# Unequal chunks in a fused Mamba and mixture-of-experts kernel, and zero rows only where they are read

## The chip, the cores and the metric

The kernel runs on one core of one Trainium2 chip. The metric is device time in microseconds (us). A core has five engines with queues of their own: TensorE (PE, matrix products; its weight loads are listed as PEld), VectorE (DVE), ScalarE (ACT), GpSimd (POOL) and SyncE (SP), which issues most of the DMA transfers here. An engine works through its own instructions in order and waits for others at semaphores. SBUF is the on-chip memory with 128 partitions, PSUM the small memory into which PE writes.

## What is computed

The input `x` is 4 sequences of 1024 tokens of 256 values. Two layers follow, each with a residual and a layer norm. The first is a selective state-space layer (512 channels, 16 states per channel), the second a mixture of experts: one shared expert for all tokens, and 8 experts of which each token takes the best 2.

```python
# first layer: x = layernorm(x + attn(x)), where attn adds x once more
h = x * rsqrt(mean(x * x) + EPS) * norm_scale
xs, res = split(h @ w_in, 2)                   # 2 x 512 channels
res = silu(res)
xs = silu(causal_depthwise_conv(xs, conv_w, conv_b))   # 4 taps
delta, B, C = split(xs @ w_xproj, [16, 32])
delta = softplus(delta @ w_dt + b_dt)
deltaA = exp(delta[..., None] * A)
deltaBx = (delta * xs)[..., None] * B[:, :, None, :]
ys = scan over tokens: ys[t] = deltaA[t] * ys[t - 1] + deltaBx[t]
out = (einsum('blcn,bln->blc', ys, C) + xs * D) * res
x = layernorm(x + (x + out @ w_out))
# second layer: x = layernorm(x + ffn(x))
normed = x * rsqrt(var + 1e-08) * norm_weight
shared = relu(normed @ sw1 + sb1) @ sw2 + sb2
probs = sigmoid(flat @ router_w.T)
scores, idx = top_k(probs, 2)                  # of 8; weights: scores over their sum
routed = sum over the two experts e of weight * (relu(flat @ ew1[e] + eb1[e]) @ ew2[e] + eb2[e])
x = layernorm(x + shared + routed)
```

## The kernel before

**Chunks.** A sequence is cut into chunks (b, c) of `TC` = 512 tokens, eight in all. Each goes through three stages.

`front` (line 248) normalises the tokens, turns them so that channels lie on partitions (`hT`), projects them (`pi`), convolves (line 298 on ACT, then three taps each for four channel blocks on DVE, line 304), and works out `delta`, `xs * delta` and the rows of B and C (`parts`). For the second chunk of a sequence, the last three columns of the chunk before come in through `halo`.

The scan runs one state n at a time, 16 steps for a chunk (the loop from line 926). A step has these parts: `inputs` multiplies `xs` by B (DVE line 406 for three channel blocks, POOL line 410 for the fourth); for each of four channel blocks k, `scan` lets ACT make `da` (line 418) in one of two PSUM buffers, and DVE scans along the tokens (line 421), from zero or from the state that `keep` saved; `outputs` multiplies by C (DVE line 434) and adds up over n (POOL line 435).

`tail` (line 438) multiplies by the gate, projects back (`po`, line 458), adds the residual, normalises, writes the result to the DRAM array `sums`, and routes: the router's product, the top two of eight and their weights. `by_expert` then counts with two matrix products where each token's row belongs, and POOL scatters rows (values, weight, token number) into the DRAM array `rows` with indirect DMAs (line 596), where each expert has a stretch of its own. Last it makes a `plan`: which experts have full blocks of 128 rows, and where they begin. `channels` marks a chunk whose shared work can begin, `routes` one whose plan is there.

**Units of expert work.** `units` (line 662) is a fixed list: for each chunk one unit for each 128 tokens of the shared expert, then `BLOCKS` routed units. How many tokens each expert has is not known when the program is built, so the numbers are those that any routing can fill: 1, 8, 8, 8, 8, 8, 8, and for the last chunk the rest, 22. With the shared ones, four for each chunk, that makes 103. A unit loads its expert's weights (two of 1 MB, `need`, two buffers each), its rows (`load_rows`, line 713; rows after an expert's last token must hold zeros and a harmless token number), turns them, multiplies by the first weights (`up`, line 768), takes Relu on ACT (line 777), multiplies by the second (`down`, line 798), and adds its 128 rows into `sums` with an indirect DMA (line 830). Which expert, and where its rows begin, are read from `plan` into SyncE's registers (lines 695 and 722). `fill` writes zero rows over all of `rows` once, 1806 KB in each DMA, beginning at step 2 of the first chunk.

**Order.** The order in which instructions enter the queues is written out by hand with Python generators. `front` of the next chunk and `tail` of the one before are advanced by `side()`, twice in each step; that is 32 turns in a chunk, whatever its length. Expert work `moe()` (line 838) is advanced by `other_work()` 0.85 times for each k, four k to a step; a unit takes four turns (two in `up`, two in `down`), and the `up` of a unit comes ahead of the `down` of the one before. Turns that find nothing ready are lost. After the last scan the remaining units run with two turns to each turn of the last tail, and `finish` (line 873) normalises `sums` and writes the output.

Of the kernel before, what the change touches and what calls it, by code (L numbers as in the profile page):

```python
# [22 lines left out]
TC = 512  # L23
NCH = SEQ // TC
TT = TC // P
# [14 lines left out]
GROUP = NSEQ * NCH  # L40
NGROUP = NSEQ * NCH // GROUP
CAP = GROUP * TC
FULL = TC * TOPK // BS


BLOCKS = [FULL * k + FULL - (E - 1) for k in range(GROUP - 1)] + [FULL * GROUP + E - 1]
BLOCKS = [after - (BLOCKS[k - 1] if k else 0) for k, after in enumerate(BLOCKS)]
NB = max(BLOCKS)
# [3 lines left out]
NS = NB * BS + E * CAP  # L52
# [5 lines left out]
def mamba_moe_kernel(  # L58
# [32 lines left out]
    def load_x(b, c):  # L91
        t = two.tile([P, TT, D], F32, tag="x", name=f"x_{b}_{c}", bufs=3)
        nc.sync.dma_start(t, x[b, c * TC : (c + 1) * TC, :].rearrange("(t p) d -> p t d", p=P))
        return t
# [62 lines left out]
    nc.vector.tensor_scalar(starts, steps[:, 0:E], float(CAP), float(NB * BS), ALU.mult, ALU.add)  # L157
# [11 lines left out]
    halo = const.tile([P, KB, K - 1], F32, tag="halo", name="halo")  # L169


    rows_of, sums_of = [], []
    for g in range(NGROUP):
        rows_of.append(dram.tile([NS, W], F32, tag=f"rows{g}", name=f"rows{g}", bufs=1))
        sums_of.append(dram.tile([P + GROUP * TC, D], F32, tag=f"sums{g}", name=f"sums{g}", bufs=1))

    empty = one.tile([P, W], F32, tag="o", name="empty")
# [5 lines left out]
    def fill(g):  # L183

        nc.sync.dma_start(sums_of[g][0:P, :], empty[:, 0:D])
        rows = rows_of[g].rearrange("(n p) d -> p n d", p=P)
        for n in range(0, NS // P, 14):
            some = min(14, NS // P - n)
            nc.sync.dma_start(
                rows[:, n : n + some, :], empty.unsqueeze(1).to_broadcast([P, some, W])  # L190
            )
            yield
# [23 lines left out]
    def to_channels(hn, which, dst, name):  # L216

        for k in range(KD):
            pt = ps_mix.tile([P, TC], F32, tag="mix", name=f"pt_{name}_{k}")
            for t in range(TT):  # L220
                nc.tensor.transpose(
                    pt[:, t * P : (t + 1) * P], hn[:, t, k * P : (k + 1) * P], ident
                )
            yield
            nc.scalar.activation(
                dst[:, k, :], pt, AF.Identity, scale=norms_sb[:, which, k : k + 1]
            )
# [15 lines left out]
    chunks = [(b, c) for b in range(NSEQ) for c in range(NCH)]  # L243

    sofar_of, done_of = {}, {}


    def front(b, c):
        s = f"{b}_{c}"
        x_sb = xs_in[b, c]  # L250
# [44 lines left out]
        for k in range(KB):  # L295
# [5 lines left out]
            )  # L301
            for back in range(1, K):
# [4 lines left out]
            if c + 1 < NCH:  # L307
                nc.scalar.copy(halo[:, k, :], pi[:, TC - (K - 1) :])
            yield
        if c > 0:  # L310
            come = one.tile([P, KB, K - 1], F32, tag="come", name=f"come_{s}")
# [76 lines left out]
    def over_partitions(step, row):  # L388

        b, c, n = step  # L390
        pb = ps_mix.tile([P, TC], F32, tag="mix", name=f"pb_{b}_{c}_{row}")
# [8 lines left out]
    def inputs(step, pb):  # L400
        b, c, n = step
        xs = scans[b, c][0]
# [10 lines left out]
    def scan(step, hs, of):  # L413
        b, c, n = step
        delta = scans[b, c][1]
# [10 lines left out]
    def keep(step, hs):  # L426
        b, c, n = step
        if c + 1 < NCH:
            nc.scalar.copy(state[:, :, n : n + 1], hs[:, :, TC - 1 : TC])  # L429

    def outputs(step, hs, pb):
        b, c, n = step
        y = scans[b, c][2]
        nc.vector.tensor_tensor(hs, hs, pb.unsqueeze(1).to_broadcast([P, KB, TC]), ALU.mult)  # L434
# [3 lines left out]
    def tail(b, c):  # L438
        s = f"{b}_{c}"
        g, at = divmod(chunks.index((b, c)), GROUP)  # L440
        own_sums = sums_of[g][P + at * TC : P + (at + 1) * TC, :]
# [35 lines left out]
        for _ in range(3):  # L477
# [4 lines left out]
            base=P + at * TC, channel_multiplier=1,  # L482
# [3 lines left out]
        yield  # L486
        x1T = one.tile([P, KD, TC], F32, tag="x1T", name=f"x1T_{s}")
# [3 lines left out]
        pr = ps_mix.tile([P, TC], F32, tag="mix", name=f"pr_{s}")  # L491
# [13 lines left out]
        den, flat = part(TT), part(TT * E * E)  # L505
# [18 lines left out]
        tie = flat.rearrange("p (t e f) -> p t e f", t=TT, e=E)  # L524
# [26 lines left out]
        if at:  # L551
            nc.gpsimd.tensor_copy(sofar[:, 0, :], sofar_of[g][:, TT, :])
        else:
            nc.gpsimd.memset(sofar[:, 0, :], 0.0)
        sofar_of[g] = sofar
# [9 lines left out]
        yield from by_expert(b, c, hn, rank, weights, both, part, flat)  # L565

    def by_expert(b, c, hn, rank, weights, both, part, flat):

        s = f"{b}_{c}"
        g, at = divmod(chunks.index((b, c)), GROUP)  # L570
        blocks, last_of_group = BLOCKS[at], at == GROUP - 1
# [3 lines left out]
        nc.tensor.matmul(place, lhsT=ones, rhs=sofar_of[g], start=True, stop=False)  # L575
# [17 lines left out]
        def scatter(i):  # L593
            nc.gpsimd.tensor_copy(hn[:, :, WEIGHT : WEIGHT + 1], weights[:, i, :].unsqueeze(2))
            for t in range(TT):
                ins = nc.gpsimd.indirect_dma_start(  # L596
                    rows_of[g][:, :],
# [5 lines left out]
                for other in taken_from[g]:  # L603
                    tc.declare_no_dep(ins, other, reason="rows behind those of full blocks")
                scatters.append(ins)


        if not at:
            done_of[g] = one.tile([P, E], F32, tag="done", name=f"done_{g}")
            nc.gpsimd.memset(done_of[g], 0.0)  # L610
        done = done_of[g]
        levels = [P, E, CAP // BS]
        over = one.tile(levels, F32, tag="ahead", name=f"over_{s}")
        level = full_at[:, 0 : CAP // BS] if last_of_group else full_at[:, 1:]
        nc.vector.tensor_tensor(
            over, counts.unsqueeze(2).to_broadcast(levels),
            level.unsqueeze(1).to_broadcast(levels), ALU.is_gt if last_of_group else ALU.is_ge,
# [9 lines left out]
        base, ends, first, whose, first_of = part(E), part(E), part(E), part(blocks), part(blocks)  # L627
        nc.vector.tensor_reduce(base, ee, AX.X, ALU.add)
# [19 lines left out]
        nc.vector.tensor_reduce(first_of, of, AX.X, ALU.add)  # L648
        plan = two.tile([P, 2, blocks], I32, tag="plan", name=f"plan_{s}")
        nc.vector.tensor_scalar(plan[:, 0, :], whose, float(E - 1), None, ALU.min)  # L650
        nc.vector.scalar_tensor_tensor(
            plan[:, 1, :], step, float(BS), first_of, ALU.mult, ALU.add
        )
        if not last_of_group:
# [8 lines left out]
    for i, (b, c) in enumerate(chunks):  # L663
        units += [(b, c, SHARED, j) for j in range(TC // BS)]
        units += [(b, c, None, j) for j in range(BLOCKS[i % GROUP])]
# [6 lines left out]

    def group(u):
        return chunks.index(units[u][0:2]) // GROUP
# [36 lines left out]
    blocks_in, rows_in, taken_from = {}, {}, [[] for _ in range(NGROUP)]  # L711
# [3 lines left out]
    def load_rows(u):  # L715
# [4 lines left out]
        g = group(u)  # L720
# [3 lines left out]
        ins = nc.sync.dma_start(xb, rows_of[g][bass.ds(first, BS), :]).ins  # L724
# [6 lines left out]
        taken_from[g].append(ins)  # L731
# [58 lines left out]
    def down(u, hidden):  # L790
        b, c, e, j = units[u]
        g, at = divmod(chunks.index((b, c)), GROUP)
# [11 lines left out]
        if e is not None:  # L804
# [4 lines left out]
            )  # L809
            if j % 2 == 0:  # L810
# [3 lines left out]
            if j % 2:  # L814
                first = P + at * TC + (j - 1) * BS

                def add():
                    nc.gpsimd.dma_start(
                        sums_of[g][first : first + 2 * BS, :].rearrange("(t p) d -> p t d", p=P),
# [9 lines left out]
        def add():  # L829
            nc.gpsimd.indirect_dma_start(  # L830
                sums_of[g][:, :],
# [6 lines left out]
    def moe():  # L838

        while not ready(0):  # L840
            yield False
        ahead = []
        for _ in up(0, ahead):
            yield True
        for u in range(last):
            while u + 1 < last and not ready(u + 1):
                while pending:
                    pending.pop(0)()
                yield False
# [23 lines left out]
    def finish(g):  # L873

        while pending:
            pending.pop(0)()
# [145 lines left out]
```

## Time and profile before

| | us |
|---|---|
| median of 3 runs | 1759.77 (1757.38 to 1762.43) |
| the profiled execution | 1759.7 |
| its span | 1758.0 |
| start of the first scan instruction | 71.7 |
| start of the first scan of each later chunk | 224.9, 406.7, 574.4, 754.7, 935.3, 1115.5, 1291.1 |
| end of the last scan instruction | 1452.2 |
| end of the last unit's `down` | 1703.6 |
| busy: PE, DVE, ACT, POOL | 1266.4, 1285.8, 1098.3, 1159.2 |

The profile is of one execution. A group line gives the source line, engine, operation, what is written and read with its shape, how often, then the busy time of the group, the mean length of one in ns, and the idle time of the engine just before these instructions, with what ended it. A stretch line gives a window from the span's start, its length, the busy time of each engine in it, TensorE's granted clock, the DMA engines' share and their GB/s. The length of an instruction is not the distance to the next: neighbours on one engine overlap by some 0.1 us.

### The profile page before, as it was taken

What the parts mean: (1) busy time and instruction counts of PE and PEld (TensorE: products, weight loads), DVE (VectorE), ACT (ScalarE), POOL (GpSimd) and SP (SyncE); (2) the same over time, 40 slices, a digit from 0 to 9 for tenths busy, and PEclk for the clock granted to TensorE, in tenths of its full rate; (3) what the DMA queues carried; (4) which work ended last, traced back from release to release, by engine and by line L of the source; (5) the groups of instructions that cost most, each with busy time, mean ns of one, the idle gap of its engine ahead of it and who ended that gap; (6) DMA issues with size and microseconds to landing.
All of it is one profiled execution on the core that took longest, in us unless ns stands there. A gap on an engine that the chain in (4) does not pass through costs nothing.

```text
span 1758.0 us, 20275 instructions
## 1 busy us (share of the span) xinstructions
PE 1266.4 (72%) x6366; PEld 968.6 (55%) x6366; DVE 1285.8 (73%) x1369; ACT 1098.3 (62%) x2413; POOL 1159.2 (66%) x901
## 2 busy tenths in 40 slices
PE   4254245874677788788777977898788788999970
PEld 1011022652256657675566655776567677899960
DVE  2499889889998897999888979897989892100003
ACT  5557636684688587857775778677866663344433
POOL 1565876697678877996688768966897683312222
PEclk9575566786789998899988988899789899999995
DMA  9990000220115551564246524651555276599974
GB/s 295 323 318 31 0 5 20 68 68 0 27 50 163 150 158 45 153 179 143 64 142 169 167 61 123 190 156 46 160 168 156 55 233 190 153 313 319 331 234 159
DMA packets 199998, 254.18 MB, mean 145 GB/s; under 512 B 21306, under 2 KB 177091, under 8 KB 199891
## 3 DMA queue, kind: packets, MB, share of 16 engines
q1 hardware_dynamic: 173858, 222.54, 39.8%
q0 software_dynamic: 17648, 21.96, 7.0%
q10 hardware_dynamic: 8384, 8.39, 1.4%
q8 instruction: 50, 0.82, 0.2%
q14 instruction: 58, 0.47, 0.1%
HBM read 185.67 MB, written 67.20 MB: 144 GB/s over the span
## 4 chain that ended last, share of the span: by engine, by line
PE 16%; DVE 12%; POOL 9%; issue 6%; DMA 4%; ACT 3%; ACTq 0%; SPq 0%; POOLq 0%; DVEq 0%
PE pu L768 7%; PE pd L798 6%; DVE hs L421 6%; POOL y L435 3%; DMA sums<-rb,xb 2%; DVE hs L434 2%; DVE hs L406 2%; PE po L458 2%; POOL rows L596 1%; POOL hs L410 1%; DVE xs L304 1%; DMA sums<-rs 1%; POOL delta L377 1%; DMA rows<-hn,to 1%; ACT h L777 1%
## 5 line engine op out<-in xcount | busy, mean ns | idle before, releaser
L435 POOL TENSOR_TENSOR y<-y,hs 128x2048 f32<-128x2048 f32 x128 | 592.7, 4631 | 139.3 <-DVE hs L434 127.9
L418 ACT ACTIVATE da<-delta,chan_sb 128x512 f32<-128x512 f32 x512 | 352.9, 695 | 175.9 <-DVE hs L421 170.7
L798 PE MATMUL pd<-w,h 128*128 128x256 f32 x1648 | 402.4, 388 | 19.8 <-ACT rs L813 11.2
L798 PEld LDWEIGHTS pd<-w,h 128*128 128x128 f32 x1648 | 310.5, 195 | 92.5 <-issue 27.3
L421 DVE TENSOR_TENSOR_SCAN hs<-da,state,hs 128x512 f32<-128x512 f32 x256 | 317.9, 1269 | 27.7 <-ACT da L418 27.4
L421 DVE TENSOR_TENSOR_SCAN hs<-da,hs 128x512 f32<-128x512 f32 x256 | 302.9, 1208 | 28.2 <-ACT da L418 24.1
L768 PEld LDWEIGHTS pu<-xT,w 128*128 128x128 f32 x2272 | 287.0, 202 | 64.5 <-ACT xT L751 39.9
L777 ACT ACTIVATE h<-pu,wb 128x128 f32<-128x128 f32 x824 | 237.0, 368 | 121.9 <-PE pu L768 117.4
L768 PE MATMUL pu<-xT,w 128*128 128x128 f32 x2272 | 290.9, 286 | 22.7 <-ACT xT L751 21.9
L434 DVE TENSOR_TENSOR hs<-hs,pb 128x2048 f32<-128x2048 f32 x128 | 290.4, 2268 | 6.1 <-ACT state L429 4.6
L406 DVE TENSOR_TENSOR hs<-xs,pb 128x1536 f32<-128x1536 f32 x128 | 222.0, 1735 | 33.2 <-POOL xs L383 17.8
L830 POOL DMA_INDIRECT sums<-rb,xb x71 | 112.4, 1584 | 185.1 <-ACT xT L751 49.6
L392 PE MATMUL pb<-parts,pick 128*128 128x512 bf16 x256 | 108.8, 430 | 172.0 <-DVE hs L406 80.6
L410 POOL TENSOR_TENSOR hs<-xs,b 128x512 f32<-128x512 f32 x128 | 177.4, 1390 | 64.7 <-ACT b L404 63.6
L274 PE MATMUL pi<-hT,w_in_sb 128*128 128x512 f32 x256 | 151.6, 724 | 48.9 <-DVE hs L434 18.0
L768 PEld LDWEIGHTS pu<-x1T,w 128*128 128x128 f32 x1024 | 152.7, 230 | 32.8 <-issue 16.6
L768 PE MATMUL pu<-x1T,w 128*128 128x128 f32 x1024 | 158.8, 317 | 12.8 <-ACT h L777 12.8
L213 DVE BATCH_NORM_STATS2 bnst_l<-o 128x6 f32<-128x256 f32 x32 | 11.9, 412 | 190.8 <-DMA o<-sums 190.8
L274 PEld LDWEIGHTS pi<-hT,w_in_sb 128*128 128x128 f32 x256 | 52.8, 224 | 134.4 <-issue 47.3
L458 PE MATMUL po<-w_out_sb,y 128*128 128x256 f32 x256 | 78.6, 474 | 47.7 <-POOL y L447 42.0
L392 PEld LDWEIGHTS <-pick 128*128 128x128 bf16 x256 | 27.1, 107 | 133.3 <-issue 83.4
L458 PEld LDWEIGHTS po<-w_out_sb,y 128*128 128x128 f32 x256 | 61.6, 246 | 70.5 <-POOL y L447 49.1
(161 smaller groups left out, 1418.3 us busy)
## 6 DMA issues: line engine op xcount, KB each, us to landing
w<-in_ew SPq DMA_DIRECT2D x142, 1024.0 KB
rows<-empty SPq DMA_DIRECT2D x19, 1806.0 KB
w<-in_sw SPq DMA_DIRECT2D x16, 1024.0 KB
xb<-rows SPq DMA_DIRECT2D x71, 129.0 KB
x<-in_x SPq DMA_DIRECT2D x8, 512.0 KB
sums<-summed ACTq DMA_DIRECT2D x8, 512.0 KB
sums<-rs POOLq DMA_DIRECT2D x16, 256.0 KB
o<-sums SPq DMA_DIRECT2D x4, 1024.0 KB
```

Source lines behind the costliest of these rows:

```text
L274: nc.tensor.matmul(pi, lhsT=w_in_sb[:, k, m * P : (m + 1) * P], rhs=hT[:, k, :], start=(k == 0), stop=(k == KD - 1),)
L392: nc.tensor.matmul(pb, lhsT=pick[:, row : row + 1].to_broadcast([P, P]), rhs=scans[b, c][3], start=True, stop=True,)
L406: nc.vector.tensor_tensor(hs[:, 0:on_pool, :], xs[:, 0:on_pool, :], pb.unsqueeze(1).to_broadcast([P, on_pool, TC]), ALU.mult,)
L410: nc.gpsimd.tensor_tensor(hs[:, on_pool, :], xs[:, on_pool, :], copy, ALU.mult)
L418: nc.scalar.activation(da, delta[:, k, :], AF.Exp, scale=chan_sb[:, k, CA + n : CA + n + 1])
L421: nc.vector.tensor_tensor_scan(hs[:, k, :], da, hs[:, k, :], 0.0 if c == 0 else state[:, k, n : n + 1], ALU.mult, ALU.add,)
L434: nc.vector.tensor_tensor(hs, hs, pb.unsqueeze(1).to_broadcast([P, KB, TC]), ALU.mult)
L435: nc.gpsimd.tensor_tensor(y, y, hs, ALU.add)
L458: nc.tensor.matmul(po[:, i, :], lhsT=y[:, k, t * P : (t + 1) * P], rhs=w_out_sb[:, k, :], start=(k == 0), stop=(k == KB - 1),)
L768: nc.tensor.matmul(pu[:, i, :], lhsT=w[:, k, at : at + P], rhs=xT[:, k, :], start=(k == 0), stop=(k == KD - 1),)
L777: nc.scalar.activation(t[:, i, :], pu[:, i, :], AF.Relu, bias=wb[:, m : m + 1])
L798: nc.tensor.matmul(pd, lhsT=hidden[h][:, i, :], rhs=w[:, m, :], start=(m == 0), stop=(m == HB - 1 and e is None),)
```

## The change

- Chunks have lengths of their own: 256, 256, 512 in the first sequence, 512, 512 in the second and third, 512, 256, 256 in the last. There are ten. Tiles, loops and views take the chunk's length. `BLOCKS` becomes 0, 1, 8, 8, 8, 8, 8, 8, 4, 18. The sum with the shared units stays 103. `halos` has two buffers, and the halo copy stands ahead of the DVE taps.
- `fill` writes only one block of zero rows (for units that have none) and the padding rows of `sums`. After the last chunk's counts are known, eight DMAs write 128 zero rows each behind each expert's last row, at places that SyncE reads from `gaps`. Each expert's stretch has 128 rows more (`STRIDE`).
- A chunk without routed blocks scatters its rows and makes no plan. A plan's unused units point to the first block (`there_is`).
- `other_work` is advanced by 0.85 times the chunk's share of 512 for each k. `moe` begins the next unit's `up` ahead only if that unit is ready, and does not hold the present one back for it. A tail makes its `x1T` only when the shared units of the chunk before have been emitted (`shared_left`).
- `load_x` for chunk place + 2 stands in the middle of chunk `place`; before, that for place + 1 stood at its beginning.

```diff
+CHUNKS = [(256, 256, 512), (512, 512), (512, 512), (512, 256, 256)]
+LEN, FIRST = {}, {}
+for _b, _lens in enumerate(CHUNKS):
+    for _c, _len in enumerate(_lens):
+        LEN[_b, _c], FIRST[_b, _c] = _len, sum(_lens[:_c])
+MAXC = max(LEN.values())
...
-BLOCKS = [FULL * k + FULL - (E - 1) for k in range(GROUP - 1)] + [FULL * GROUP + E - 1]
-BLOCKS = [after - (BLOCKS[k - 1] if k else 0) for k, after in enumerate(BLOCKS)]
-NB = max(BLOCKS)
+BLOCKS, _so_far = {}, 0
+for (_b, _c), _len in LEN.items():
+    _blocks = (_b * SEQ + FIRST[_b, _c] + _len) * TOPK // BS
+    _after = max(_blocks - (E - 1), 0) if _blocks < TOKENS * TOPK // BS else _blocks + E - 1
+    BLOCKS[_b, _c], _so_far = _after - _so_far, _after
+NB = max(BLOCKS.values())
...
-    def fill(g):
-
-        nc.sync.dma_start(sums_of[g][0:P, :], empty[:, 0:D])
-        rows = rows_of[g].rearrange("(n p) d -> p n d", p=P)
-        for n in range(0, NS // P, 14):
-            some = min(14, NS // P - n)
-            nc.sync.dma_start(
-                rows[:, n : n + some, :], empty.unsqueeze(1).to_broadcast([P, some, W])
-            )
-            yield
+    def fill():
+
+        nc.sync.dma_start(rows_of[0:BS, :], empty)
+        nc.sync.dma_start(sums_of[0:P, :], empty[:, 0:D])
...
+            if c + 1 < len(CHUNKS[b]):
+                nc.scalar.copy(halos[:, c % 2, k, :], pi[:, TC - (K - 1) :])
             for back in range(1, K):
...
-            if c + 1 < NCH:
-                nc.scalar.copy(halo[:, k, :], pi[:, TC - (K - 1) :])
...
+        while shared_left:
+            yield
+        shared_left.extend(range(TC // BS))
         x1T = one.tile([P, KD, TC], F32, tag="x1T", name=f"x1T_{s}")
...
+        if last_chunk:
+
+            gaps = one.tile([P, E], I32, tag="gaps", name="gaps")
+            nc.vector.tensor_tensor(gaps, counts, starts, ALU.add)
+            for e in range(E):
+                where = nc.sync.value_load(gaps[0:1, e : e + 1], min_val=BS, max_val=NS - BS)
+                ins = nc.sync.dma_start(rows_of[bass.ds(where, BS), :], empty).ins
...
+        if not blocks:
+            scatter(0)
+            yield
+            scatter(1)
+            routes[b, c] = (scatters, None)
+            return
...
+        nc.vector.tensor_scalar(there_is, whose, float(E), float(BS), ALU.is_lt, ALU.mult)
+        nc.vector.tensor_tensor(there_is, step, there_is, ALU.mult)
...
-        while not ready(0):
-            yield False
-        ahead = []
-        for _ in up(0, ahead):
-            yield True
+        hidden = {}
         for u in range(last):
-            while u + 1 < last and not ready(u + 1):
-                while pending:
-                    pending.pop(0)()
-                yield False
+            if u not in hidden:
+                while not ready(u):
+                    while pending:
+                        pending.pop(0)()
+                    yield False
+                hidden[u] = []
+                for _ in up(u, hidden[u]):
+                    yield True
...
-            if u + 1 < last:
-                for _ in up(u + 1, ahead):
+            if u + 1 < last and ready(u + 1):
+                hidden[u + 1] = []
+                for _ in up(u + 1, hidden[u + 1]):
                     yield True
...
-    def other_work():
+    def other_work(share):
         nonlocal owed
-        owed += at_once
+        owed += at_once * share
...
-                        if place + 1 < len(chunks):
-                            xs_in[chunks[place + 1]] = load_x(*chunks[place + 1])
...
+                if n == N // 2 and place + 2 < len(chunks):
+                    xs_in[chunks[place + 2]] = load_x(*chunks[place + 2])
...
-            other_work()
+            other_work(LEN[b, c] / MAXC)
```

## The prediction

> **What bounds the kernel now.** I first read the 40 slices of the page: VectorE (DVE) is at 8 or 9 tenths up to slice 32, then nearly idle, and TensorE (PE) is at 9 only after that. So there are two regimes: a scan that DVE carries, then a stretch of expert work that PE carries. I then looked up the first and last scan instruction (line 421) of each chunk in the timeline and asked for busy time between those points. One row per stretch; the columns are length, busy time of PE, its weight loads, DVE, ACT, POOL, then clock and DMA:
>
> ```profile
> 72.00:225.00 153.00, 56.29 (x88) 16.64 (x86) 145.08 (x115) 88.84 (x150) 100.93 (x38) 0.59 0.45 134
> 225.00:407.00 182.00, 113.22 (x402) 73.93 (x403) 160.29 (x162) 111.72 (x209) 128.90 (x108) 0.73 0.13 39
> ...
> 574.00:755.00 181.00, 146.59 (x757) 116.31 (x756) 160.08 (x163) 130.78 (x285) 146.88 (x108) 0.90 0.45 133
> ...
> 1115.00:1291.00 176.00, 149.04 (x755) 116.78 (x754) 155.23 (x160) 125.38 (x277) 140.08 (x89) 0.89 0.45 133
> 1291.00:1452.00 161.00, 132.15 (x739) 111.18 (x738) 144.93 (x141) 100.53 (x230) 128.68 (x84) 0.90 0.51 150
> 1452.00:1704.00 252.00, 242.21 (x1608) 223.06 (x1606) 16.31 (x49) 105.52 (x345) 64.52 (x67) 0.99 0.85 262
> 1704.00:1758.00 54.00, 0.00 (x0) 0.00 (x0) 15.21 (x72) 17.20 (x37) 12.72 (x57) 0.54 0.50 158
> ```
>
> The first five rows shown are scans of one chunk of 512 tokens: DVE is busy all but 8 us of the first, 22, 21, 21 and 16 us of the others. In the sixth, PE is busy 242 of 252 us. In the last only the final norm runs. Before 72 us the first chunk's front runs alone. So the span is 72 + 1380 + 252 + 54 = 1758 us, and the profiled execution took 1759.7 (1.7 us lie outside the span), which is the median, 1759.77, within 0.1 us.
>
> Inside the scan I read two of its steps in the DVE timeline (start, length, instruction):
>
> ```profile
> 95.25 2.26 DVE L434 TENSOR_TENSOR hs<-hs,pb 128x2048 f32<-128x2048 f32 x1
> 97.43 2.33 DVE L421 TENSOR_TENSOR_SCAN hs<-da,hs 128x512 f32<-128x512 f32 x2
> 99.68 1.73 DVE L406 TENSOR_TENSOR hs<-xs,pb 128x1536 f32<-128x1536 f32 x1
> 101.33 2.33 DVE L421 TENSOR_TENSOR_SCAN hs<-da,hs 128x512 f32<-128x512 f32 x2
> 103.57 2.26 DVE L434 TENSOR_TENSOR hs<-hs,pb 128x2048 f32<-128x2048 f32 x1
> ```
>
> From start to start a step costs 2.18 + 2.25 + 1.65 + 2.24 = 8.3 us, 133 us for 16 steps. From the groups of instructions by shape (count, busy us, mean ns, idle before):
>
> ```profile
> L418 ACT ACTIVATE da<-delta,chan_sb 128x512 f32<-128x512 f32 x512 | 352.9, 695 | 175.9 <-DVE hs L421 170.7 <-issue 1.6 <-ACT summed L236 0.9
> L421 DVE TENSOR_TENSOR_SCAN hs<-da,state,hs 128x512 f32<-128x512 f32 x256 | 317.9, 1269 | 27.7 <-ACT da L418 27.4
> L421 DVE TENSOR_TENSOR_SCAN hs<-da,hs 128x512 f32<-128x512 f32 x256 | 302.9, 1208 | 28.2 <-ACT da L418 24.1 <-POOL hs L410 3.5
> L777 ACT ACTIVATE h<-pu,wb 128x128 f32<-128x128 f32 x824 | 237.0, 368 | 121.9 <-PE pu L768 117.4 <-ACT b L404 1.4 <-issue 1.1
> ```
>
> A scan that takes up a state costs 61 ns more. Last, the chain of waits in the PE stretch:
>
> ```profile
> 1685.05 3.57 PE pu L768 x32
> ...
> 1692.30 3.57 PE pu L768 x32
> ```
>
> One routed unit of expert work (a block of 128 rows) comes every 7.25 us there.
>
> **Step 1, the zero rows: 0 us.** Twenty large writes `rows<-empty`, 36.7 MB, go. They land by 135 us, beside the first chunk's scan, where DVE lacks 8 us in all, mostly behind ACT. The first scatter into these rows is at 325 us. Nothing waits for them; the bound is a gain of those 8 us.
>
> **Step 2, lead-in: -24 us.** The first front shrinks to 256 tokens. On its chain to the first scan at 72 us, these pieces scale with tokens: squares and scaling 3.4, transposes and hT 3.4, projection and convolution 13.2, Silu 1.9, pp 5.7, the pz loop 12.3, Ln 1.9, delta on POOL 4.5, y 2.6, xs on POOL 4.5, the first inputs 3.4: 57 us. Half is 28; less 4 for per-instruction cost that does not shrink. Bounds -20 and -26.
>
> **Step 3, DVE work in the scan: +39 us.** Two 512 chunks become four of 256, so 128 steps become 160, on the engine that bounds. Lengths 2048 and 1536 start 2.18 and 1.65 us apart: 1.035 ns an element and 0.06 us fixed. The trace has scans of one length only; pure proportion gives 0.56 us at 256, ACT's fixed share (below) 0.69; I take the elementwise 0.06, so 0.59, as the same engine does it. A short step is then 1.12 + 0.86 + 4 x 0.59 = 4.34 us, 69.4 for 16, against 66.6 for half a long chunk: +11 for four. Two more short chunks take up state: 128 x 0.06 = +8. Fronts: the first row's 145 less 133 is 12 us for a long front; a short one 7.4 (half, and fixed parts). Before, seven long fronts lie in the scan, after it six long and three short: +10. Tails: the chunk without a front has 145 - 137 = 8; a short one, mostly tiny router operations, 6. Seven long against six long and three short: +10. Sum 39; bounds 30 and 65 (scans at 0.69).
>
> **Step 4, DVE's waits: +29 us.** In the first and last sequence DVE now lacks 8 + 22 + 21 + 16 = 67 us. These waits come with events of a front or tail (ACT's convolution input 29 us over the run, POOL's xs 18, the router's POOL step 19), and with ACT's `da` (51). The events become more: nine fronts for seven. And ACT has less slack: from 695 and 368 ns, 0.85 ns an element and 0.26 us fixed, so `da` at 256 costs 0.48 us, 64 of them 8.5 us more than half. In chunk (3,1), with a long chunk's tail, a short front and 6.8 units of experts, I sum ACT to 31 `da` + 10 copies + 22 experts + 9 tables + 20 front and tail = 92 us, beside DVE's 89. I put the waits at 8, 19, 20 and 20, 17, 12 us in the six chunks: 96, so +29. Bounds: nothing, if waits shrink with the chunk, and +70, if ACT and DVE mostly fail to overlap in short chunks.
>
> A rule speaks against short chunks here. The row: 59 table loads on ACT at 1283 ns (7.4 a chunk); at 28.20 us one starts right after the instruction before it, and the Silu starts at 29.50, so a switch costs 1.30 us. The Trainium skill, "ScalarE: Activation LUTs", section "What ACT_TABLE_LOAD costs", adds a drain of 1380 ns, about 2.66 us for each switch. Fifteen more loads are 19 us of ACT by the row, 40 by the rule; in (3,1) ACT would stand at 102 us, above DVE, and the sum would rise by some 20 us. The row decides: 1.30.
>
> **Step 5, the end: -20 us.** The last chunk has 2 + 18 units for 4 + 22, but all 103 are still done, and how many lie before the scan's end is a matter of turns: a unit takes four, a long chunk gives 64 x 0.85 = 54, a short one 27. Following the generators' yields, 70 units are done before and 72 after. That is two, not six: chunk (3,0)'s twelve come ready halfway through (3,1), behind six of (2,1), and five of them and all six of (3,1) are left too. Two units are 14.5 us; the last tail's PE work (32 `po` matmuls, transposes, router: 12 us) halves, -6. Bounds -28 and -8.
>
> **Step 6, waits added: +1 us.** The eight gap writes need SyncE register loads that wait for `gaps` from DVE; queued behind on SyncE are the weight loads of the next units. Two buffers of each weight are two units, 14.5 us, of cover; 8 x (0.57 load + 0.4 issue) = 8 us fit. Without the cover 8 us, once. The last chunk's row loads wait for these writes, but already waited for scatters (until 1531 us), and there are four scatters instead of eight. Shared weights for two more chunks are 4 MB, at a DMA share of 0.45. The check on `shared_left` holds back (3,1)'s tail two steps, with experts to do. The earlier load of x saves only 2.9 us of ACT wait, seen once, at the start. The halo copy ahead of the taps, the unit that no longer waits for its successor, and one more small DVE operation a chunk: within 2 us together.
>
> Sum: -24 + 39 + 29 - 20 + 1 = +25, on 1759.7: **1785 us**.
>
> **Rivals.** A (0.52): as summed; 1770 to 1805. B (0.20): DVE's waits are a share of time, not of events; step 4 gives +3, the total 1759. For it: many waits are for token-sized work (POOL's 4.6 us `y`). Against: chunks with a tail lose 20 us whatever their neighbours. C (0.20): in (0,1), which carries a long front, and (3,1), ACT, DVE and POOL near 90 us each come one after another in place of beside; +70 in step 4, total 1826 at most, 1812 likely. D (0.08), the faster side: the waits halve in short chunks, because each is the remainder of a token-sized POOL or ACT operation. Then 3 + 9 + 19 and 19 + 9 + 7 = 66, no growth; with lead-in -26, end -25 and DVE at +36, the total is 1745. It decides where DVE's idle time in these six chunks stays under 70 us. That the change does not do what it says can show only in the end stretch: if 32 units or more are left after the last scan, as now, step 5 is zero.
>
> **How the numbers follow.** About 0.3%, 5 us, is what a measurement can tell from no change. A and C are slower; B is split, two parts in three within 5 us or faster; D is faster. Faster 0.10, same 0.12, slower 0.78. The range reaches from B and part of D to most of C: 1754 to 1813.
>
> **What would show it.** Right: first scan at 48 us; `rows<-empty` down to small writes; scans of 256 near 0.67 us long; chunk (3,1) near 106 us and (0,1) near 110; last scan near 1496; 30 or 31 units after it. Wrong: DVE idle under 70 us in the six chunks, scans of 256 far from 0.67 us, or an end stretch under 215 us.

## The result: slower by 3.5%, and the profile after

The kernel before takes 1758.58 us (median), the changed one 1820.94: ratio 1.0354 [1.0331, 1.0377]. The direction was forecast; the time lies 36 us above the forecast of 1785 and 8 above the range. The profiled execution has a span of 1817.8 us. The rows below are the stretches of the changed kernel, one row for each of its ten chunks from first scan to first scan, then from the last scan to the last unit, and the final norm (columns as before):

```profile
50.50:137.30 86.80, 33.94 (x83) 16.72 (x82) 76.35 (x114) 59.01 (x146) 55.03 (x43) 0.58 0.00 0
137.30:251.80 114.50, 65.44 (x222) 36.83 (x223) 92.50 (x142) 81.37 (x182) 76.05 (x82) 0.71 0.10 23
251.80:424.00 172.20, 87.34 (x273) 47.62 (x272) 160.92 (x160) 104.38 (x184) 120.98 (x92) 0.71 0.10 29
424.00:598.50 174.50, 119.60 (x530) 80.83 (x530) 156.73 (x165) 120.15 (x249) 134.33 (x96) 0.81 0.25 75
598.50:785.90 187.40, 153.04 (x745) 118.29 (x745) 166.85 (x164) 127.68 (x276) 140.24 (x105) 0.86 0.42 126
785.90:971.10 185.20, 148.54 (x761) 114.51 (x760) 160.38 (x165) 132.37 (x298) 145.94 (x104) 0.90 0.45 132
971.10:1155.40 184.30, 149.07 (x742) 114.72 (x741) 161.69 (x164) 126.66 (x271) 142.44 (x106) 0.87 0.42 124
1155.40:1321.50 166.10, 135.44 (x732) 112.70 (x733) 150.15 (x164) 117.25 (x285) 134.90 (x106) 0.90 0.46 137
1321.50:1439.60 118.10, 91.93 (x513) 76.31 (x511) 92.54 (x164) 84.68 (x231) 89.58 (x88) 0.88 0.43 125
1439.60:1534.10 94.50, 76.32 (x438) 63.56 (x437) 79.00 (x138) 66.78 (x176) 66.23 (x70) 0.91 0.49 146
1534.10:1763.10 229.00, 222.21 (x1465) 203.30 (x1464) 12.23 (x47) 95.52 (x314) 55.13 (x58) 0.99 0.90 279
1763.10:1817.80 54.70, 0.00 (x0) 0.00 (x0) 15.20 (x72) 17.50 (x37) 12.82 (x57) 0.52 0.50 156
```

The same stretches of both kernels (us; "lead-in" is the time to the first scan, and the middle is the second and third sequence):

| stretch | before | after | difference | forecast |
|---|---|---|---|---|
| lead-in | 71.7 | 50.5 | -21.2 | -24 |
| first sequence | 335.0 | 373.5 | +38.5 | +68 with the last |
| four chunks in the middle | 708.8 | 731.4 | **+22.6** | **0** |
| last sequence | 336.7 | 378.7 | +42.0 | (above) |
| last scan to last unit | 251.4 | 229.0 | -22.4 | -20 |
| final norm | 54.4 | 54.7 | +0.3 | 0 |

The differences sum to the 59.8 us between the spans. The surprise is the third row: those chunks have 512 tokens in both kernels. The short steps are as forecast. In the DVE timeline of chunk (0,0):

```profile
79.21 0.94 DVE L410 TENSOR_TENSOR hs<-xs,pb 128x768 f32<-128x768 f32 x1
80.07 1.21 DVE L438 TENSOR_TENSOR hs<-hs,pb 128x1024 f32<-128x1024 f32 x1
81.20 1.26 DVE L425 TENSOR_TENSOR_SCAN hs<-da,hs 128x256 f32<-128x256 f32 x2
82.38 0.45 DVE L308 SCALAR_TENSOR_TENSOR xs<-pi,chan_sb,xs 128x255 f32<-128x255 f32 x1
```

From start to start these are 0.86, 1.13 and 2 x 0.59 us, where 0.86, 1.12 and 0.59 were taken. The groups by shape (count, busy us, mean ns, idle before):

```profile
L425 DVE TENSOR_TENSOR_SCAN hs<-da,state,hs 128x256 f32<-128x256 f32 x192 | 136.5, 736 | 27.7 <-ACT da L422 16.9 <-POOL hs L414 8.4 <-POOL y L439 1.9
L422 ACT ACTIVATE da<-delta,chan_sb 128x256 f32<-128x256 f32 x256 | 120.1, 479 | 37.4 <-DVE hs L425 35.3
L425 DVE TENSOR_TENSOR_SCAN hs<-da,hs 128x256 f32<-128x256 f32 x64 | 41.2, 675 | 6.7 <-ACT da L422 6.5
```

Scan, 61 ns for the state, and `da` at 0.48 us are the forecast's figures. In the end stretch's chain the units are 7.25 us apart, as before:

```profile
1693.78 3.57 PE pu L789 x32
...
1701.03 3.57 PE pu L789 x32
```

The zero rows are gone: nine writes of 129 KB in place of 36.7 MB. In the middle, DVE's largest wait has grown. First the changed kernel, then, by the same view, the kernel before (line waited for, us, times, longest):

```profile
DVE hs L425 <- ACT da L422: 43.0, 19, 5.0
```

```profile
DVE hs L421 <- ACT da L418: 26.3, 18, 3.8
```

That is not all of it, as DVE's busy time there has grown too, from 632.1 to 645.7 us, though its work is the same. Part of this is standing that the profile counts as work. In the timeline of the changed kernel:

```profile
667.07 4.52 POOL L439 TENSOR_TENSOR y<-y,hs 128x2048 f32<-128x2048 f32 x1 [5.35 <-DVE hs L438]
...
668.68 2.93 DVE L200 TENSOR_SCALAR root_r<-half_r 128x4 int32<-128x4 int32 x1
```

The operation on four elements a partition lasts here until POOL's `y` ends at 671.6. Its group, and that of the operation ahead of it (min, median, longest in ns), show that such lengths are the exception:

```profile
L198 DVE TENSOR_SCALAR half_r<-ms x10: 141/160/4499, 5.0 to 1216.9; 128x4 int32<-128x4 int32 x6, 128x2 int32<-128x2 int32 x4
L200 DVE TENSOR_SCALAR root_r<-half_r x10: 135/163/2986, 5.2 to 1226.5; 128x4 int32<-128x4 int32 x6, 128x2 int32<-128x2 int32 x4
```

I call DVE instructions of at most 64 elements a partition that last over 1 us "standing" and add them up for the four middle chunks (us):

| kernel | length | DVE's other work | standing | idle | of it for `da` |
|---|---|---|---|---|---|
| before | 708.8 | 629.1 | 3.0 | 76.7 | 26.3 |
| after | 731.4 | 632.7 | 12.9 | 85.7 | 43.0 |
| order alone (e4, below) | 727.5 | 633.1 | 5.9 | 88.5 | 42.8 |
| change, order held (f4) | 682.0 | 630.2 | 11.1 | 40.7 | 19.1 |
| equal, held (g1) | 711.4 | 632.7 | 11.3 | 67.4 | 25.5 |
| equal, held, plan mended (h2) | 709.4 | 633.1 | 3.0 | 73.4 | 26.4 |
| first short, held, plan mended (i1) | 687.8 | 629.3 | 12.5 | 45.9 | 21.5 |

The work is the same everywhere, within 4 us. Of the 22.6 us, standing has 9.9 and idle time 9.0. Which edits did it is the question for the runs; how much of the standing is a cost of its own is seen at h2.

### The profile page after: what moved, and what is told of

Same layout as the page of the kernel before. It is cut to its first block, busy times and chain, and to the rows that moved or that the text cites. A ratio compares the mean times of both kernels' runs of the same rounds, so it can differ in the third digit from the quotient of the medians.

```text
span 1817.8 us, 21573 instructions
## 1 busy us (share of the span) xinstructions
PE 1298.7 (71%) x6534; PEld 994.7 (55%) x6534; DVE 1335.6 (73%) x1679; ACT 1164.6 (64%) x2721; POOL 1192.6 (66%) x1066
## 4 chain that ended last, share of the span: by engine, by line
PE 19%; POOL 17%; DVE 14%; issue 8%; DMA 5%; ACT 4%; SPq 0%; POOLq 0%; ACTq 0%; DVEq 0%
POOL y L439 7%; PE pd L818 7%; PE pu L789 7%; DVE hs L425 6%; DVE hs L438 3%; DMA sums<-rb,xb 3%; PE po L463 2%; DVE hs L410 2%; POOL hs L414 2%; POOL sums L851 1%; POOL y L452 1%; POOL rows L604 1%; ACT da L422 1%; DMA sums<-rs 1%; POOL delta L380 1%
## 5 line engine op out<-in xcount | busy, mean ns | idle before, releaser
L439 POOL TENSOR_TENSOR y<-y,hs 128x2048 f32<-128x2048 f32 (+1 forms) x160 | 603.2, 3770 | 167.0 <-DVE hs L438 152.0
L422 ACT ACTIVATE da<-delta,chan_sb 128x512 f32<-128x512 f32 (+1 forms) x640 | 385.3, 609 | 157.5 <-DVE hs L425 153.6
L818 PE MATMUL pd<-w,h 128*128 128x256 f32 x1648 | 423.3, 401 | 39.4 <-ACT h L798 22.4
L425 DVE TENSOR_TENSOR_SCAN hs<-da,state,hs 128x256 f32<-128x256 f32 (+1 forms) x384 | 374.7, 1002 | 53.1 <-ACT da L422 42.0
L438 DVE TENSOR_TENSOR hs<-hs,pb 128x2048 f32<-128x2048 f32 (+1 forms) x160 | 294.9, 1843 | 16.5 <-ACT state L433 13.7
L425 DVE TENSOR_TENSOR_SCAN hs<-da,hs 128x512 f32<-128x512 f32 (+1 forms) x256 | 268.8, 1075 | 39.3 <-ACT da L422 33.4
L798 ACT ACTIVATE h<-pu,wb 128x128 f32<-128x128 f32 x824 | 236.5, 370 | 88.1 <-PE pu L789 76.7
L396 PE MATMUL pb<-parts,pick 128*128 128x512 bf16 (+1 forms) x320 | 120.8, 380 | 196.8 <-DVE hs L410 90.6
L410 DVE TENSOR_TENSOR hs<-xs,pb 128x1536 f32<-128x1536 f32 (+1 forms) x160 | 226.2, 1414 | 30.4 <-POOL y L439 13.0
L414 POOL TENSOR_TENSOR hs<-xs,b 128x512 f32<-128x512 f32 (+1 forms) x160 | 190.9, 1197 | 68.5 <-ACT b L408 65.7
L276 PE MATMUL pi<-hT,w_in_sb 128*128 128x512 f32 (+1 forms) x320 | 159.1, 630 | 43.7 <-DVE hs L438 13.7
L408 ACT COPY b<-pb 128x512 f32<-128x512 f32 (+1 forms) x160 | 80.7, 505 | 57.2 <-PE pb L396 51.2
```

Of the source, the lines that this page charges most:

```text
L276: nc.tensor.matmul(pi, lhsT=w_in_sb[:, k, m * P : (m + 1) * P], rhs=hT[:, k, :], start=(k == 0), stop=(k == KD - 1),)
L396: nc.tensor.matmul(pb, lhsT=pick[:, row : row + 1].to_broadcast([P, P]), rhs=scans[b, c][3], start=True, stop=True,)
L410: nc.vector.tensor_tensor(hs[:, 0:on_pool, :], xs[:, 0:on_pool, :], pb.unsqueeze(1).to_broadcast([P, on_pool, TC]), ALU.mult,)
L414: nc.gpsimd.tensor_tensor(hs[:, on_pool, :], xs[:, on_pool, :], copy, ALU.mult)
L422: nc.scalar.activation(da, delta[:, k, :], AF.Exp, scale=chan_sb[:, k, CA + n : CA + n + 1])
L425: nc.vector.tensor_tensor_scan(hs[:, k, :], da, hs[:, k, :], 0.0 if c == 0 else state[:, k, n : n + 1], ALU.mult, ALU.add,)
```

## The experiments

Ratios are to the kernel before, with 95% intervals; "middle" is the four middle chunks, 709 us before.

**Which edit.** Theory 1 was that edits without a size cost the middle its 22 us; the rival, that the short chunks push the middle too. Four runs take the change apart: all edits with equal chunks; short chunks in the first, or the last, sequence alone; and the kernel before with the new `moe` alone.

```diff
-CHUNKS = [(256, 256, 512), (512, 512), (512, 512), (512, 256, 256)]
+CHUNKS = [(512, 512)] * 4                                             # e1
+CHUNKS = [(256, 256, 512), (512, 512), (512, 512), (512, 512)]        # e2
+CHUNKS = [(512, 512), (512, 512), (512, 512), (512, 256, 256)]        # e3
```

> All edits of the change, but eight equal chunks of 512 as before. Theory 1 (the four long chunks in the middle, which lost 22 us in the changed kernel, lose them to the other edits: the order of the expert work, the halo copy, the router's extra operations): every chunk loses some 5 us here too, 1758 + 8 x 5 = 1798 us, between 1785 and 1805. Rival (the short chunks push the middle too, by shifting what lies beside what): nothing of it here, 1753 to 1765 us.

1791.11 us, 1.0165 [1.0127, 1.0202]; middle 735. This is in the range of theory 1: about half of the net loss is there with equal chunks. Its middle has 20.6 us of standing.

> All edits, but only the first sequence has short chunks (256, 256, 512). By the trace of the changed kernel the first scan starts 21 us sooner and the first sequence's scan takes 38 us more: +17. Theory 1 adds some 5 us for each of the six other chunks: 1758 + 17 + 30 = 1805 us. The rival (short chunks push the middle) gives 1758 + 17 + 22 = 1797, with the last sequence as before. Short chunks that cost nothing but the two terms: 1775.

1818.6 us, 1.0305 [1.0267, 1.0343]; middle 735. This is above both expectations.

> All edits, but only the last sequence has short chunks (512, 256, 256). By the trace of the changed kernel the last sequence takes 42 us more and the end stretch 22 less: +20. Theory 1 adds 5 us for each of the six chunks ahead: 1758 + 20 + 30 = 1808 us. The rival gives the middle nothing, since no short chunk lies ahead of it: 1778.

1795.19 us, 1.0182 [1.0146, 1.0217]. This lies between the two expectations, but the middle takes 728 us though no short chunk lies ahead of it, which speaks against the rival. With this order a short beginning costs 27 us over e1, a short end 4.

> The kernel before with one edit: the expert generator does not hold a unit back for its successor, and begins the next unit ahead only when it is ready. If this edit is what the middle chunks lose time to: 1775 to 1798 us. If the halo copy or the router's operations are: within 5 us of 1758. If it helps, because the last unit of a chunk is not held back: 1745 to 1753.

1790.03 us, 1.0158 [1.012, 1.0196]; middle 727.5, with 42.8 us of waits for `da`, as in the changed kernel (43.0). The order alone loses about what e1 loses:

```profile
DVE hs L421 <- ACT da L418: 42.8, 21, 5.3
```

Of the 30 us between its span and that of the kernel before, 19 lie in the middle (12 of them idle time of DVE), 7 in the last sequence and 5 behind the last scan.

**Undoing the order.** In the new order a chunk's last routed unit finishes at once, and the `up` of the next chunk's first shared unit no longer lies ahead of its `down`. Holding it back again, with all else of the change kept (the old order also held a chunk's last shared unit; this edit does not):

```diff
         for u in range(last):
...
+            while units[u][2] is None and u + 1 < last and not ready(u + 1):
+                while pending:
+                    pending.pop(0)()
+                yield False
             for v in range(u + 1, u + 3):
```

> The whole change, but the last routed unit of a chunk is again held back until the next chunk's first unit is ready. If the expert order is worth its 28 us here too: 1821 - 28 = 1793 us, 1784 to 1800, which is the forecast's sum for the short chunks. If the short chunks have a phase of their own, in which the order does not matter: 1810 to 1825.

1770.96 us, 1.0059 [1.0038, 1.008]: 50 us less than the change, more than the 28 that were expected. First and last sequence and the end stretch keep their lengths within some 4 us each; the middle falls from 731 to 682:

```profile
426.00:590.30 164.30, 116.75 (x493) 77.48 (x494) 154.65 (x165) 117.73 (x238) 132.16 (x96) 0.82 0.24 73
590.30:766.10 175.80, 146.71 (x781) 116.47 (x780) 165.64 (x166) 128.42 (x285) 146.61 (x107) 0.92 0.47 140
766.10:934.60 168.50, 140.65 (x724) 108.37 (x725) 155.86 (x163) 127.37 (x287) 139.07 (x101) 0.92 0.46 137
934.60:1108.00 173.40, 144.06 (x781) 113.97 (x780) 165.14 (x166) 127.10 (x279) 146.76 (x107) 0.94 0.48 141
```

```profile
DVE hs L425 <- ACT da L422: 19.1, 11, 3.3
```

DVE's idle time there is 41 us for 86, with work and standing within 3 us of the change's. So what the order costs here is waiting, and the wait that shrinks most is the one for `da`, 43.0 to 19.1.

The same with equal chunks, and with only the last sequence short:

> All edits of the change with the held unit put back, and eight equal chunks of 512. Theory S (the short chunks cost what the steps of the forecast say, some +19 in the first and +17 in the last sequence by the trace of the run with both; the other edits help the middle by 27 us): 1771 - 36 = 1735 us, 1725 to 1745, below the kernel before. Rival (the middle is fast only because short chunks lie before it): 1755 to 1765, and the short chunks cost 9 us in all.

1761.38 us, 1.0007 [0.9995, 1.0019]. The time is the rival's, not theory S's 1735. The order costs 30 us with equal chunks, 50 with short ones.

> The same, with short chunks in the last sequence alone. Theory S: 1735 + 17 = 1752 us, 1742 to 1760. Rival: as the kernel before, 1758 to 1770.

1781.81 us, 1.0146 [1.0102, 1.0191]: above both expectations, and more than with both ends short. The prices of the two ends don't add up.

**Is it the place?** On e4's kernel two empty turns between the two `up`s, or ahead of the first; on the kernel before, the same two turns after the hold:

```diff
+                if u:
+                    yield True
+                    yield True
```

> The kernel before with the new expert order, and two turns left empty after the first unit's up in each chunk, where the old order had the held unit's down. All later units then stand at the same steps as in the old order; only the held unit itself is done early. Theory P (the new order is slow because everything after stands two turns, 0.6 of a step, sooner): back to 1755 to 1766 us. Theory H (the held unit's down fills PE where the next chunk's first units wait for ACT and for weights): stays at 1782 to 1795, or grows, as two turns more are lost.

1779.53 us, 1.0108 [1.0081, 1.0136]. The middle is back at 701 us, but the last chunk takes 180.5 us for 161, 14.0 of it waits for `da`.

> The same two empty turns, but ahead of the first unit's up. Theory P: like the other, 1755 to 1768 us. Theory H: 1782 to 1800. If only the distance between the first unit's up and the second's counts (ACT must clear two PSUM buffers in between): this one stays slow, 1780 or more, and the one with the gap in between gets fast.

1781.45 us, 1.0105 [1.0078, 1.0132]; middle 711, last chunk again 180.6. Both times lie between theory P and theory H, this one at the edge of H.

> The kernel before, old order, with two empty turns after each hold: all expert work after it stands two turns later. If the time depends on where the turns fall among the steps (the kernel sits at a good place, and any shift costs): 1770 to 1795 us, like the new order. If the step at which expert work stands does not matter: 1758, plus at most 2 units more after the last scan, 1758 to 1768.

1759.02 us, 0.9986 [0.9971, 1.0001]. Two turns later, the old order loses nothing.

The share of turns instead, 0.80 for 0.85, on e4's kernel and on the whole change:

> The kernel before with the new order of the units alone, and 0.80 instead of 0.85 of a turn per scan. With 0.85 it took 1790 us, the middle chunks 727 instead of 709. If the share was only set for the old order, the middle falls to about 709 and the time to 1765 to 1775, the later units costing some 10 us at the end. If the units' places are what costs, whatever the share, the time stays at 1780 to 1795.

1776.48 us, 1.0104 [1.0078, 1.013]; middle 712, as the first expectation had it, the time 1 us above its range.

> The whole change as it is, with 0.80 instead of 0.85 of a turn per scan of 512. If the 50 us come from where the units stand among the other work, the time moves by more than 10 us, as it did on the kernel before (1790 to 1776): 1790 to 1810. If they come with the order whatever the places, 1816 to 1826.

1834.26 us, 1.0418 [1.038, 1.0457]: by more than 10 us, but upwards, a miss of both expectations. Its middle stays at 730.5 us; the last sequence takes 384 for 379 and the stretch from last scan to last unit 236 for 229. So on the kernel before, the new order costs 18 to 20 us in three other places and 28 in its own; inside the change, later places leave the middle alone and cost at the end. No simple lateness explains it.

**The other edits.** The halo copy ahead of the taps, and the earlier `load_x`, each on the kernel before, then both:

```diff
+            if c + 1 < NCH:
+                nc.scalar.copy(halo[:, k, :], pi[:, TC - (K - 1) :])
             for back in range(1, K):
...
-            if c + 1 < NCH:
-                nc.scalar.copy(halo[:, k, :], pi[:, TC - (K - 1) :])
```

> The kernel before with one edit, the halo copy on ACT ahead of the three DVE taps, so that ACT does not wait for DVE there. If this is the edit that makes the middle 27 us faster: 1730 to 1745 us. If not, 1753 to 1763, as PE and ACT waited for it some 4 and 28 us in all, off the critical engine.

1745.8 us, 0.9926 [0.9904, 0.9947]: 14 us faster. In the kernel before, the copy was the last to read `pi`, behind the taps, and PE waited for it before it overwrote the buffer:

```profile
PE pi L274 <- ACT halo L308: 12.2, 4, 5.5
```

With the copy first, PE waits for the taps instead, 17.6 for 14.7 us, and all its waits for `pi` come to 45.3 for 49.0; DVE's for the convolution input fall from 28.8 to 23.9. So these waits account for part of the 14 us only. In the profile the first and the last sequence are each 7 us shorter, the middle only 2: this edit is not what shortens f4's middle.

> The kernel before with one edit, the load of x for the chunk after next in the middle of a chunk. If this is the edit that makes the middle faster: 1730 to 1745 us. If not, 1753 to 1763: ACT waited 2.9 us for x, once.

1751.89 us, 0.9952 [0.9935, 0.9969]: 8 us faster, between the two expectations.

> The kernel before with the halo copy ahead of the taps and with x of the next chunk asked for half a chunk sooner; all else as before. If the two gains have separate causes (14 us for the copy, 8 us for x, each measured alone), the time is 1735 to 1741. If both only reshuffle the queues, they need not add up: 1742 to 1756, as one of them alone or less.

1744.41 us, 0.9921 [0.9898, 0.9945]. That is what the copy gains alone: the two gains do not add up.

**A small operation that is not small.** g1 has the halo copy first and yet gains nothing. The clearest case of standing is in its timeline:

```profile
698.47 4.51 POOL L439 TENSOR_TENSOR y<-y,hs 128x2048 f32<-128x2048 f32 x1
698.48 0.16 DVE L677 TENSOR_SCALAR plan<-pr 128x8 int32<-128x8 f32 x1
698.54 0.69 ACT L422 ACTIVATE da<-delta,chan_sb 128x512 f32<-128x512 f32 x1 [3.30 <-DVE hs L425]
698.60 5.63 DVE L675 TENSOR_TENSOR there_is<-steps,there_is 128x8 f32<-128x8 f32 x1
...
702.93 1.26 POOL L414 TENSOR_TENSOR hs<-xs,b 128x512 f32<-128x512 f32 x1
...
704.14 1.74 DVE L410 TENSOR_TENSOR hs<-xs,pb 128x1536 f32<-128x1536 f32 x1
```

A DVE operation on 8 elements a partition takes 5.63 us. It reads two tiles of SBUF, begins 0.13 us after POOL's `y`, and ends at 704.2 when POOL's next one has ended too. Four times of eight in g1 it takes 5.2 to 6.7 us, and no list of waits names it:

```profile
L675 DVE TENSOR_TENSOR there_is<-steps,there_is x8: 166/2707/6732, 334.4 to 1527.6; 128x8 f32<-128x8 f32 x6, 128x1 f32<-128x1 f32 x1, 128x22 f32<-128x22 f32 x1
```

With a PSUM operand in each instruction, and one instruction fewer:

```diff
-        nc.vector.tensor_scalar(there_is, whose, float(E), float(BS), ALU.is_lt, ALU.mult)
-        nc.vector.tensor_tensor(there_is, step, there_is, ALU.mult)
+        nc.vector.scalar_tensor_tensor(there_is, whose, float(E), step, ALU.is_lt, ALU.mult)
...
-        nc.vector.tensor_tensor(plan[:, 1, :], first_of, there_is, ALU.add)
+        nc.vector.scalar_tensor_tensor(
+            plan[:, 1, :], there_is, float(BS), first_of, ALU.mult, ALU.add
+        )
```

> All edits, equal chunks, the last routed unit held back, and the planning operation with two SBUF inputs replaced by one with a PSUM input. Without the edit this kernel took 1761 us, with four such operations of 5.2 to 6.7 us (about 23 us of VectorE together). If VectorE stands there because GpSimd's instruction and it both read SBUF, the operations fall to about 0.2 us and the time to 1738 to 1750. If VectorE would have waited there in any case, the operations fall and the time stays at 1757 to 1765. If the long time has another cause, the operations stay at 5 us.

1749.77 us, 0.9946 [0.9923, 0.997]: 12 us less than g1. Its group is

```profile
L674 DVE SCALAR_TENSOR_TENSOR there_is<-pr,steps x8: 141/148/180, 333.0 to 1511.3; 128x8 f32<-128x8 f32 x6, 128x1 f32<-128x1 f32 x1, 128x22 f32<-128x22 f32 x1
```

(min, median, longest in ns). The Trainium skill, "SBUF — State Buffer", section "Who interferes with whom", says that a DVE instruction with two SBUF inputs contends with a GpSimd instruction that reads SBUF; the edit's effect agrees. Standing is not all cost, though: in the middle it falls from 11.3 to 3.0 us, but DVE's idle time rises from 67.4 to 73.4 and the length falls by 2 us only. Where the rest of the 12 us lies the profiles cannot say well, as g1's is of its slowest execution (1770.68 us).

> The whole change with its own chunks, the last routed unit held back, and the same planning edit. Without it this kernel took 1771 us. The operation stands less often here (the profile of after has it long once in four): 1762 to 1771 if the standing is what costs, 1771 and above if it is covered.

1771.07 us, 1.0073 [1.0045, 1.0101]: nothing gained, as this operation takes 1.2 us at most in f4.

**The best version.** All edits, order held, planning mended, only the beginning short:

> All edits with the last routed unit held back and the planning edit, short chunks in the first sequence only. With equal chunks this kernel took 1750 us, with both ends short 1771, and there the four middle chunks took 686 us together instead of 705. If lead-in (21 us won) and first sequence (some 38 lost) are all that changes, 1765 to 1770. If the middle chunks come out short here too, because it is the short beginning that shifts them, 1742 to 1752.

1743.95 us, 0.9908 [0.9877, 0.994], faster than both kernels, and level with the halo copy alone. Its first sequence loses 40 us to the kernel before (375 for 335); its lead-in wins 21, its middle 21 (688) and its last sequence 16 (321 for 337). Why a short beginning, under the held order, cuts DVE's idle time in the middle from 73 us (h2) to 46 is not settled.

## Why the prediction was wrong, step by step

- **Step 1 (zero rows, 0 us): right** as far as the profiles go; no run isolates it. The first chunk's scan, beside which the writes lay, takes 152.9 us in e1 and 153.3 in g1, which do without them, and 153.2 before.
- **Step 2 (lead-in, -24): right**, -21.2.
- **Step 3 (DVE's work, +39): right in kind, 7 us low.** DVE is busy 651.5 us in the six chunks for 605.5 in their four, +46, of which 4 are more standing. The scans cost what was taken.
- **Step 4 (waits, +29): right in size.** DVE's idle time there is 10.4 + 22.0 + 11.3 + 16.0 + 25.6 + 15.5 = 101 us, where 96 was put; 67 before, so +34. The spread over the chunks was not foreseen: more in (0,1) and (3,1), less in (0,2); so (3,1) took 118 us where 106 was put. And the size is right in part by luck: e1, with equal chunks and the change's other edits, has only 60 us of idle time in these two sequences, so against it the short chunks added 41. The row of the table load held: 75 loads for 59, `da` 1.30 us after the start of one (331.33, 332.63). ACT is busy 84.7 us in (3,1), DVE 92.5, so the longer switch that the prediction weighed, with ACT at 102, is not what made this chunk long.
- **Step 5 (end, -20): right**, -22.4, with 30 units left.
- **Step 6 is the step that failed**: "The halo copy ahead of the taps, the unit that no longer waits for its successor, and one more small DVE operation a chunk: within 2 us together." Alone on the kernel before, the copy is worth -14 us and the unit +28 (+50 inside the change); the small operation costs 12 us in g1. They do not cancel. That "within 2 us together" was put without working. With it went the unsaid premise that the four middle chunks keep their 709 us; they take 727 to 735 in after, e1, e2, e3 and e4, all with the new order and 0.85, and 682 to 712 in every kernel with the old order.

So steps 2 to 5 come to +37 us where the forecast had +24 (-21.2 + 80.5 - 22.4), and the middle adds 22.6. Rivals B and D fell with step 4. C's time, 1812 to 1826, is what was measured, but its mechanism is not: (0,1) and (3,1) do lose 22 and 26 us, yet the waits grew by 34 and not 70, and the rest came where no chunk is short.

**What is shown and what is open.** Shown: the new order of the units costs 28 to 50 us, and holding the last routed unit back takes this back. In the middle this is mostly idle time of DVE (12 of 19 us between before and e4, 45 of 49 between f4 and the change), and the wait that changes most is that for `da` (by 16.5 and 23.9 us). Not shown is why the order costs more beside short chunks, and why f4's middle is 27 us shorter than before. What puts ACT behind is only argued: `da` stands in one queue with the units' Relus, copies and the chunk's tail, and where these meet depends on every instruction ahead. That two turns restore the middle and lose 19 us in the last chunk, and that 0.80 helps one kernel and hurts the other, fits this and proves no particular chain. I found none that holds in all of e4, f1 and i2.

## What to carry to other kernels

Where several engines share hand-ordered queues, an edit that only changes which unit stands first is not free until it has been run alone; bound its gain by the idle time of the bounding engine in every stretch that it touches (here 77 us in the middle, where "within 2 us" was put for three edits together), and allow for a loss as well. A bundle with one good reason should be taken apart before it is judged: two of its small edits gained 14 us together, one lost 28 to 50. Look in the busy time of an engine for tiny operations that are long: beside GpSimd work a PSUM operand in place of one in SBUF took one kind of them away here, which was worth 12 us in one kernel and nothing in another.

## What had not been expected of the hardware

A 128 x 8 operation with two SBUF operands took 5.2 to 6.7 us in g1, 5.63 beside GpSimd in the case shown, and 0.17 us at its shortest. In that case it ended with the second of two GpSimd instructions in succession, not with the first. Operations on four integers with one SBUF input (`half_r`, `root_r`) stood for up to 4.5 and 3.0 us as well, in the changed kernel.
